# A two-layer graph kernel: layer 1 from the neighbour lists runs without a branch, and a branch behind it computes layer 1 from all of adj where the lists do not hold

## The chip, the core and the metric

One core of a Trainium2 chip runs one program. Its engines are PE (TensorE, matrix products), DVE (VectorE), ACT (ScalarE), POOL (GpSimd) and SP (SyncE, which issues DMAs here and computes nothing). Each engine runs its own instructions in a fixed order and waits at semaphores for the others; the order is what a scheduler makes of the kernel's source, except where `tc.keep_in_program_order` pins an instruction to its place in the source. The metric is device microseconds (us) of one execution, as the median of the runs.

## What is computed

4096 nodes with 512 features each, two layers. `adj` is 4096 x 4096; an entry is above zero for under 1% of the pairs, the diagonal among them, and its weights lie between 0.05 and 1.

```python
# layer 0
h = jnp.maximum(_layernorm(x, axis=-1), 0.0)
d = adj.sum(axis=1) ** -0.5            # 0 where the sum is 0
x = x + relu(((d[:, None] * adj * d[None, :]) @ h) @ W0 + b0)
# layer 1
h = jnp.maximum(_layernorm(x, axis=-1), 0.0)
g = h @ W1
e = leaky_relu(g @ a[:F] + (g @ a[F:]).T, 0.2)
pos =  softmax(where(adj > 0,  e, -1e12), axis=1)
neg = -softmax(where(adj > 0, -e, -1e12), axis=1)
x = x + elu(concatenate([pos @ h, neg @ h], axis=1) @ wtrans)
```

(The reference, written a little shorter.) Layer 1 needs for each node only the rows of h of its neighbours.

## The kernel before

**Layer 0** multiplies all of `adj` with h in dense form, in groups of row tiles of 128 nodes (`GROUPS`; `multiply_blocks`, L888 to L921, is its inner product; the rows of the profile name its matmuls L895). The last group holds the two tiles 24 and 25, called late. `finish0` (L807 to L828) finishes one tile: the residual, the layer norm with Relu on ACT (`normalize`, L640), two dot products on DVE (L818) which give the node's two score terms s and t, and `put_row`, which writes h, t and (elsewhere) the neighbour masks as a row to a table in DRAM. While layer 0 runs, DVE and POOL also make, for each block of 64 nodes, a list of all nodes that are a neighbour of one of them.

**Layer 1 from the lists** (`sparse_layer1`, from L1241 on) works on 64 blocks r of 64 nodes, two blocks to a pair n. `gather` issues indirect DMAs on POOL's queue (L457), each of which fetches 128 table rows that the lists name: a pair takes 22 of them, in three parts a = 0, 1, 2 of 8, 6 and 8 (`CHUNKS`). The even block of a pair uses parts 0 and 1, the odd block parts 1 and 2. Then per block:

- `weights`: scores s + t (DVE, L469), leaky relu (L475), exponentials of both signs (ACT, L479), masks (DVE, L486), a tree of sums over them (L491 to L497).
- `product`: 14 matmuls of 128 x 512 on PE, 28 records in the profile (L1303); the inverse sums scale the result on ACT (`us`, L1312); `turn_u` transposes it on PE (`tp`, L512).
- `finish1`, per pair: 8 matmuls with `wtrans`, 16 records (L1326), elu and residual, one store by SP (L1339).

Four to six gathers of a pair run ahead of its products, into buffers that alternate between pairs. `pause` (L447 to L451) is a copy on POOL, called `mark` in the profile, that waits until the last DMA of a gathered part has landed; it stands in the source behind part 1 of the first pair, part 0 of the second, and part 2 of the second to the sixth pair. The scheduler decides how many gathers of the next part stand between a part's own gathers and its mark.

**The early pair.** Pair 16 (blocks 33 and 32) is computed inside the last group of layer 0, before the late tiles are known: `gather0`, `weights0` and `product0` do the neighbours in the table, and `late_weights0` and `late_product0` add the late tiles' rows from SBUF. Layer 1 then begins with pair 17, whose blocks are 34 and 35.

**The verdict.** The lists have fixed lengths. `judge` (L1006 to L1032) tests whether every neighbour was listed, whether row sums are above zero and whether the scores are small enough for exponentials without a running maximum. It takes the minimum of the tests (`all_ok`), and a matmul with ones (`ok_ps`) adds it over the 128 partitions. Every engine loads the sum and branches: `sparse_layer1` where it is 128, `dense_layer1` where it isn't, which computes layer 1 from all of `adj`. For the data at hand every test holds.

The order around the seam in the source is: `weights0` of block 33 at step 10 of the last group and of block 32 at its last step; nine of the 14 chunks of block 33's product; `finish0` of the two late tiles; `judge`; the last five chunks; `spread_s`; block 32's product; the late parts; the branch; layer 1. Layer 1 opens with the load of four pairs' s (`load_s`, SP), the gathers of pairs 17 and 18, the load of `wtrans` to `wt_sb` (2 MB, SP) and, a block later, copies of table rows (SP).

Of the kernel before, what the change touches and what calls it, by code (L numbers as in the profile page):

```python
# [8 lines left out]
F32 = mybir.dt.float32  # L9
# [4 lines left out]
AF = mybir.ActivationFunctionType  # L14
ALU = mybir.AluOpType
AX = mybir.AxisListType
# [3 lines left out]
P = 128  # L20
# [239 lines left out]
def gcn_gat_kernel(  # L260
# [23 lines left out]
    nc = tc.nc  # L284
    N, F = x.shape
# [16 lines left out]
    late0, n_late = GROUPS[-1]  # L302
# [9 lines left out]
    def bank(name):  # L312
        return ps.tile([P, 512], F32, tag="ps", name=name)

    ones = const.tile([P, P], F32, name="ones")
# [154 lines left out]
            z, t.to_broadcast([P, n, RB]), s.unsqueeze(1).to_broadcast([P, n, RB]), ALU.add  # L470
        )

    def exps(z, p, bound=False):

        nc.vector.scalar_tensor_tensor(z, z, ALPHA, z, ALU.mult, ALU.max)  # L475
        if bound:
            nc.vector.tensor_scalar(z, z, 2 * MAXS, -2 * MAXS, ALU.min, ALU.max)
        for g in range(2):
            nc.scalar.activation(p[:, :, g, :], z, AF.Exp, scale=(1.0, -1.0)[g])  # L479

    def mask_out(r, p, mask):

# [38 lines left out]
    with sbuf(name="y0", bufs=1) as y_pool, sbuf(name="wa", bufs=1) as wa_pool, sbuf(name="bits", bufs=4) as bits_pool, sbuf(name="small0", bufs=4) as small, ExitStack() as rest, ExitStack() as lists:  # L521
# [108 lines left out]
        def normalize(out, xt, name, pin=False):  # L630

            mv = mean_var(small, xt, name, pin)
            r = small.tile([P, 2], F32, tag="rr", name=f"rr{name}")
            nc.vector.tensor_scalar(r[:, 0:1], mv[:, 1:2], EPS, None, ALU.add)
            nc.vector.reciprocal(r[:, 0:1], r[:, 0:1])
            nc.scalar.activation(r[:, 0:1], r[:, 0:1], AF.Sqrt)
            nc.vector.scalar_tensor_tensor(
                r[:, 1:2], mv[:, 0:1], -1.0, r[:, 0:1], ALU.mult, ALU.mult
            )
            nc.scalar.activation(out, xt, AF.Relu, bias=r[:, 1:2], scale=r[:, 0:1])  # L640

        def load_x(x_pool, queue, j):
            xs[j] = x_pool.tile([P, F], F32, tag="xt", name=f"xt{j}")
# [165 lines left out]
        def finish0(work, j, y, h, prod):  # L809

            xt = xrs.pop(j)
            nc.vector.scalar_tensor_tensor(y, y, 0.0, xt, ALU.max, ALU.add)
            nc.gpsimd.dma_start(out=x1_dram[j], in_=y)
            nc.gpsimd.memset(h[:, ROW_T + 1 :], 0.0)
            normalize(h[:, :F], y, f"b{j}")

            def dot(g, vec):
                nc.vector.scalar_tensor_tensor(  # L818
                    prod(f"prod{j}_{g}"), h[:, :F], 1.0, wa_bc[g], ALU.mult, ALU.mult, accum_out=vec
                )  # L820

            dot(1, h[:, ROW_T : ROW_T + 1])
            put_row(nc.gpsimd, tab0, j, h)
            if all(not j0 <= j < j0 + n for j0, n in GROUPS[-2:]):
                for g in others:
                    put_row(nc.scalar, g, j, h)
            dot(0, s_all[:, j : j + 1])
            nc.vector.tensor_copy(t_all[:, j : j + 1], h[:, ROW_T : ROW_T + 1])  # L828
# [176 lines left out]

        def judge():  # L1006

            ok = small.tile([P, 8], F32, tag="ok", name="ok", bufs=1)
            nc.gpsimd.memset(ok, 1.0)
            nc.vector.tensor_tensor(listed, listed, count, ALU.is_equal)  # L1010
            for g in range(2):
                nc.vector.tensor_reduce(ok[:, 4 + g : 5 + g], listed[:, g], AX.X, ALU.min)
            nc.vector.tensor_tensor(room[0], room[0], room[1], ALU.min)
            nc.vector.tensor_scalar(ok[:NH, 0:1], room[0], 0.0, None, ALU.is_ge)
            nc.vector.tensor_reduce(ok[:, 1:2], d_all, AX.X, ALU.min)
            nc.vector.tensor_scalar(ok[:, 1:2], ok[:, 1:2], 0.0, None, ALU.is_gt)
            for g, vec in enumerate((s_all, t_all)):
                sq = small.tile([P, NJ], F32, tag="sq", name=f"sq{g}", bufs=1)
                nc.vector.tensor_tensor(sq, vec, vec, ALU.mult)
                nc.vector.tensor_reduce(ok[:, 2 + g : 3 + g], sq, AX.X, ALU.max)  # L1020
                nc.vector.tensor_scalar(
                    ok[:, 2 + g : 3 + g], ok[:, 2 + g : 3 + g], MAXS * MAXS, None, ALU.is_le
                )
            all_ok = small.tile([P, 1], F32, tag="all_ok", name="all_ok", bufs=1)
            nc.vector.tensor_reduce(all_ok, ok[:, 0:7], AX.X, ALU.min)
            ok_ps = bank("ok_ps")
            tc.keep_in_program_order(
                nc.tensor.matmul(ok_ps[0:1, 0:1], all_ok, ones[:, 0:1], start=True, stop=True)
            )
            verdict = const.tile([1, 1], I32, name="verdict")  # L1030
            tc.keep_in_program_order(nc.vector.tensor_copy(verdict, ok_ps[0:1, 0:1]))
            return verdict  # L1032

        def group(b, work, at_pool, sum_pool, step, prod, n_h=2):
# [86 lines left out]
        with sbuf(name="work2", bufs=2) as work, sbuf(name="sums2", bufs=2) as sum_pool, sbuf(name="at2", bufs=4) as at_pool, sbuf(name="scratch", bufs=1) as scratch, sbuf(name="pair", bufs=1) as pair:  # L1121
            gts, ps0, totals, u0 = {}, {}, {}, {}
            blocks = (2 * PAIR0 + 1, 2 * PAIR0)
# [24 lines left out]
            def weights0(r):  # L1148
                nk = sum(CHUNKS[r % 2 : r % 2 + 2])
                z = scratch.tile([P, nk, RB], F32, tag="z", name=f"z{r}")  # L1150
                p = ps0[r] = pair.tile([P, nk + n_late, 2, RB], F32, name=f"p{r}")
                for gt, k, n in parts0(r):
                    scores(s_of0(r), z[:, k : k + n], gt[:, :, ROW_T : ROW_T + 1].bitcast(F32))
                exps(z, p[:, :nk], bound=True)
                for gt, k, n in parts0(r):
                    mask_out(r, p[:, k : k + n], gt[:, :, ROW_W:].bitcast(U8))
                q = p[:, :nk].rearrange("p k g c -> p k (g c)")
                totals[r] = tree(scratch, r, q, nk // 2, "z", 2)
# [14 lines left out]
            def product0(r, lo=0, hi=n_block):  # L1173
                if lo == 0:
                    u0[r] = bank(f"u{r}")
                for gt, k0, n in parts0(r):
                    for k in range(max(lo - k0, 0), min(hi - k0, n)):
                        i = nc.tensor.matmul(
                            u0[r],
                            ps0[r][:, k0 + k].rearrange("p g c -> p (g c)"),  # L1180
                            gt[:, k, :F].bitcast(F32),
                            start=k0 + k == 0,
                            stop=False,
                        )
                        if r == blocks[0]:
                            tc.keep_in_program_order(i)

            def late_product0(r):
                for k in range(n_late):
                    nc.tensor.matmul(  # L1190
                        u0[r],
                        ps0[r][:, n_block + k].rearrange("p g c -> p (g c)"),
                        late_h[:, k, :F],
                        start=False,
                        stop=k == n_late - 1,
                    )
                rl = inverse_sums(scratch, r, totals[r])
                u = xin.tile([P, F], F32, tag="xr", name=f"us{r}")
                nc.scalar.activation(u, u0[r], AF.Copy, scale=rl)
                turn_u(r, u, ut0)  # L1200

            def step(jp):
                if jp == 0:
                    nc.scalar.dma_start(
                        out=s_pair,
                        in_=s_dram[PAIR0 * P : (PAIR0 + 1) * P].partition_broadcast(P),
                    )
                if jp == 4:
                    gather0(1)
                if jp == 7:  # L1210
                    gather0(2)
                if jp == 10:
                    gather0(0)
                    weights0(blocks[0])
                if jp == NP - 1:
                    weights0(blocks[1])
                    warm = small.tile([P, 1], F32, tag="warm", name="warm2", bufs=1)
                    tc.keep_in_program_order(
                        nc.scalar.activation(warm, ones[:, 0:1], AF.Sqrt)
                    )  # L1220
# [4 lines left out]
                out=rows_of(tab0, late0 // EJ)[:, k : k + n_late, ROW_W:],  # L1225
                in_=late_m[:, k : k + n_late].bitcast(I32),
            )
            product0(blocks[0], hi=n_block - 5)
            for j, y in pending[1](work, row_tile).items():
                finish0(work, j, y, late_h[:, j - late0], row_tile)  # L1230
            verdict = judge()
            product0(blocks[0], lo=n_block - 5)
            spread_s(late0, n_late)
            product0(blocks[1])
            for r in blocks:
                late_weights0(r)
            for r in blocks:
                late_product0(r)


    def sparse_layer1():  # L1241
# [142 lines left out]
            turn(order[-1])  # L1384
            finish1(order[-1] // 2)

    go = nc.values_load(
        verdict[0:1, 0:1],
        min_val=0,
        max_val=P,  # L1390
        skip_runtime_bounds_check_because="a sum of 128 zeros and ones",
    )
    with tc.If(go == P) as branch:
        sparse_layer1()
    with branch.Else():
        dense_layer1(
            tc, adj_t, wtrans, out, x1_dram, table[tab0], s_all, t_all, ident, ones, load_adj_t, bank
        )
# [30 lines left out]
```

## Time and profile before

| | before |
|---|---|
| median of 3 runs | 2140.81 us (2140.43 to 2140.95) |
| profiled execution | 2128.36 us |
| its span | 2126.5 us |
| mean granted TensorE clock | 0.975 |
| DMA bytes, mean rate | 524.13 MB, 246 GB/s |

The page gives each engine's busy share over the span of one execution, a timeline, the chain of waits that ended last, and groups of instructions by line. Where the kernel's stages differ, a table of stretches of time says more than the shares: on this core layer 0 runs to about 1055 us, the early pair to about 1086 us, and layer 1 from there to the end. A group's mean hides where its instructions stand, so single instructions are read from the timeline of an engine. Its rows give the start in us, the length, the engine, the line, the operation with output and inputs, how many instructions were drawn together, and in brackets the idle time of the engine before them, with what ended it.

The costliest groups of layer 1, of the whole span:

```profile
L457 POOL DMA_INDIRECT g<-table,idx x704 | 742.6, 1055 | 261.6 <-issue 191.6
L1303 PE MATMUL u<-g,p 128*128 128x512 f32 x1736 | 764.8, 598 | 4.1 <-DVE p L486 4.1
L1326 PE MATMUL o<-wt_sb,ut 128*128 128x512 f32 x512 | 229.3, 601 | 0.5 <-ACT ut L516 0.5
```

The columns are the line, the engine, the operation and its number; busy time in us and the mean in ns; and the idle time before them with what ended most of it.

### The profile page before, as it was taken

To read this page: it belongs to the slowest core of one execution; us is meant where nothing else is said; L and a number is where in the kernel's file an instruction comes from. 1 tells how busy PE (TensorE), PEld (TensorE's weight loads), DVE (VectorE), ACT (ScalarE), POOL (GpSimd) and SP (SyncE) were. 2 spreads that over 40 slices of the span, in tenths; PEclk is the share of its full clock that TensorE was granted. 3 is DMA by queue.
4 is the path that set the end of the run, shared out by engine and by line. 5 is a ranking of instruction groups with operands and counts; after the bars stand their busy time and mean duration, and the time that the engine had idled before them with its cause. 6 is when DMAs were issued, how large, how long until landed. Compare 5 with 4: busy or idle time off the path is not lost.

```text
span 2126.5 us, 20058 instructions
## 1 busy us (share of the span) xinstructions
PE 2008.1 (94%) x6456; PEld 1184.0 (56%) x6456; DVE 1121.1 (53%) x2804; ACT 511.4 (24%) x876; POOL 915.8 (43%) x988
## 2 busy tenths in 40 slices
PE   7999899999899889899799999999999999999998
PEld 3444346888787768788544444444444444444443
DVE  5444436563797459935635435445445545445441
ACT  4645522223332310000112112122122122122120
POOL 2010001111112320321467667777777677677740
PEclk9999999999999999999899999999999999999999
DMA  9988926887887776464598878898888888888850
GB/s 373 364 313 311 347 84 231 303 274 223 309 276 256 254 241 208 129 221 136 163 309 248 251 227 257 285 296 256 276 253 264 254 271 246 237 247 241 238 167 21
DMA packets 188042, 524.13 MB, mean 246 GB/s; under 512 B 25235, under 2 KB 34419, under 8 KB 187926
## 3 DMA queue, kind: packets, MB, share of 16 engines
q0 software_dynamic: 71296, 275.22, 42.1%
q1 hardware_dynamic: 88480, 196.46, 27.1%
q10 hardware_dynamic: 28150, 51.07, 6.7%
q8 instruction: 52, 0.85, 0.2%
q14 instruction: 64, 0.52, 0.1%
HBM read 430.83 MB, written 102.92 MB: 251 GB/s over the span
## 4 chain that ended last, share of the span: by engine, by line
PE 47%; DVE 7%; DMA 5%; POOL 5%; issue 3%; ACT 1%; ACTq 0%; DVEq 0%; SPq 0%; POOLq 0%
PE u L1303 31%; PE o L1326 9%; PE p L895 5%; POOL g L457 5%; DMA g<-table,idx 2%; DMA at<-in_adj_t 2%; DVE keys L393 1%; DVE lst L391 1%; PE tp L512 1%; DMA table<-h 1%; ACT m L720 1%; DVE p L486 0%; DVE prod L818 0%; PE cs L502 0%; ACTq L443 0%
## 5 line engine op out<-in xcount | busy, mean ns | idle before, releaser
L457 POOL DMA_INDIRECT g<-table,idx x704 | 742.6, 1055 | 261.6 <-issue 191.6
L1303 PE MATMUL u<-g,p 128*128 128x512 f32 x1736 | 764.8, 598 | 4.1 <-DVE p L486 4.1
L1303 PEld LDWEIGHTS u<-g,p 128*128 128x128 f32 x1736 | 326.9, 191 | 393.3 <-issue 371.4
L469 DVE TENSOR_TENSOR z<-g,s 128x512 f32<-128x512 f32 (+1 forms) x124 | 77.4, 624 | 401.8 <-DMA g<-table,idx 365.4
L895 PE MATMUL p<-t,sums 128*128 128x256 f32 x832 | 249.4, 385 | 13.1 <-DVE sums L883 13.1
L895 PE MATMUL p<-y,sums 128*128 128x256 f32 x832 | 252.2, 385 | 6.6 <-DVE sums L885 6.6
L895 PE MATMUL p<-y,at 128*128 128x256 f32 x832 | 252.5, 386 | 2.9 <-DMA at<-in_adj_t 2.6
L1326 PE MATMUL o<-wt_sb,ut 128*128 128x512 f32 x512 | 229.3, 601 | 0.5 <-ACT ut L516 0.5
L479 ACT ACTIVATE p<-z 128x896 f32<-128x896 f32 (+2 forms) x136 | 116.0, 903 | 317.2 <-DVE z L475 287.2
L895 PEld LDWEIGHTS p<-t,sums 128*128 128x128 f32 x832 | 159.9, 193 | 37.0 <-DVE sums L883 15.0
L895 PEld LDWEIGHTS p<-y,sums 128*128 128x128 f32 x832 | 161.0, 194 | 30.1 <-DVE sums L885 7.4
L854 PE MATMUL acc<-y,at 128*128 128x512 f32 x384 | 174.9, 593 | 2.4 <-ACT y L706 2.4
L486 DVE SCALAR_TENSOR_TENSOR p<-g,p 128x384 f32<-128x384 uint8 (+1 forms) x256 | 143.4, 620 | 63.4 <-ACT p L479 60.4
L895 PEld LDWEIGHTS p<-y,at 128*128 128x128 f32 x832 | 159.2, 193 | 28.9 <-ACT m L720 3.0
L731 POOL DMA_DIRECT2D table<-m x71 | 54.1, 764 | 249.8 <-ACT m L720 145.6
L1326 PEld LDWEIGHTS o<-wt_sb,ut 128*128 128x128 f32 x512 | 96.4, 193 | 110.5 <-issue 109.8
L720 ACT ACTIVATE m<-at 128x1024 uint8<-128x1024 f32 (+1 forms) x110 | 105.2, 987 | 181.4 <-DMA at<-in_adj_t 132.7
L683 PE MATMUL yp<-w_sb,hx_t 128*128 128x512 f32 x256 | 125.0, 635 | 20.9 <-ACT y L706 18.4
L895 PE MATMUL p<-t,at 128*128 128x256 f32 x416 | 126.6, 387 | 18.9 <-DVE w L780 17.3
L1312 ACT ACTIVATE us<-u,rl 128x512 f32<-128x512 f32 x62 | 42.5, 686 | 382.2 <-issue 203.7
L854 PEld LDWEIGHTS acc<-y,at 128*128 128x128 f32 x384 | 70.5, 190 | 80.5 <-issue 77.6
L413 POOL DMA_INDIRECT ld<-li,off x48 | 43.9, 915 | 158.3 <-DMA ld<-li,off 108.1
(182 smaller groups left out, 1724.5 us busy)
## 6 DMA issues: line engine op xcount, KB each, us to landing
at<-in_adj_t SPq DMA_DIRECT2D x136, 512.0 KB, 5.4
ar<-in_adj SPq DMA_DIRECT2D x128, 512.0 KB, 8.7
table<-h ACTq DMA_DIRECT2D x182, 258.0 KB, 6.3
table<-m POOLq DMA_DIRECT2D x55, 256.0 KB, 5.5
at<-in_adj_t SPq DMA_DIRECT2D x32, 384.0 KB, 5.7
g<-table,idx POOLq DMA_INDIRECT x704, 4.2
xr<-in_x SPq DMA_DIRECT2D x32, 256.0 KB, 5.1
x<-x1d SPq DMA_DIRECT2D x32, 256.0 KB, 5.4
```

What stands on the lines that cost most here:

```text
L413: return nc.gpsimd.indirect_dma_start(out=lst_dram[g][:, :], out_offset=bass.IndirectOffsetOnAxis(ap=off[g][:, e, c : c + 1], axis=0), in_ ...
L457: nc.gpsimd.indirect_dma_start(out=gt[:, k, :], out_offset=None, in_=table[2 * n // RPT], in_offset=bass.IndirectOffsetOnAxis(ap=idx[n // ...
L469: return nc.vector.tensor_tensor(z, t.to_broadcast([P, n, RB]), s.unsqueeze(1).to_broadcast([P, n, RB]), ALU.add)
L479: nc.scalar.activation(p[:, :, g, :], z, AF.Exp, scale=(1.0, -1.0)[g])
L486: nc.vector.scalar_tensor_tensor(e, m, 0.0, e, ALU.is_gt, ALU.mult)
L683: nc.tensor.matmul(yp, hx_t[j][:, c * P : (c + 1) * P], w0_sb[:, c, :], start=c == 0, stop=c == FC - 1,)
L720: nc.scalar.activation(m, at, AF.Sign)
L731: nc.gpsimd.dma_start(out=rows_of(t, e)[:, c:, ROW_W + (a - t * TT) * P // 4 : ROW_W + (b - t * TT) * P // 4], in_=masks[i0][:, c:, (a - i ...
L854: nc.tensor.matmul(a, at[:, 0, it * P : (it + 1) * P], y0[j], start=j == 0, stop=j == NJ - 1)
L895: i = nc.tensor.matmul(out, left[:, x * P : (x + 1) * P], right, start=jp == 0 and first, stop=jp == NP - 1 and (final or not first),)
L1303: nc.tensor.matmul(u, p[:, k0 + k].rearrange("p g c -> p (g c)"), gt[:, k, :F].bitcast(F32), start=k0 + k == 0, stop=k0 + k == nk - 1,)
L1326: nc.tensor.matmul(po, ut[:, g, c, :], wt_sb[:, g * FC + c, :], start=g == 0 and c == 0, stop=g == 1 and c == FC - 1,)
```

## The change

1. `weights0` of block 32 moves from the last step of the group to behind `finish0` of the late tiles. ACT's Relu of the late tiles and its exponentials of the early pair are pinned to the source's order.
2. Block 33's product is one piece, and `judge` stands behind the early pair, unpinned. It now sums a flag for a failed test (`bad`): one more DVE instruction.
3. `sparse_layer1` runs without a branch. Behind it every engine loads the verdict, and `dense_layer1` runs where the sum is above zero; it then writes the output over.

```diff
-    def exps(z, p, bound=False):
+    def exps(z, p, bound=False, pin=False):
...
         for g in range(2):
-            nc.scalar.activation(p[:, :, g, :], z, AF.Exp, scale=(1.0, -1.0)[g])
+            i = nc.scalar.activation(p[:, :, g, :], z, AF.Exp, scale=(1.0, -1.0)[g])
+            if pin:
+                tc.keep_in_program_order(i)
...
-            normalize(h[:, :F], y, f"b{j}")
+            i = normalize(h[:, :F], y, f"b{j}")
+            if late0 <= j < late0 + n_late:
+                tc.keep_in_program_order(i)
...
-            all_ok = small.tile([P, 1], F32, tag="all_ok", name="all_ok", bufs=1)
-            nc.vector.tensor_reduce(all_ok, ok[:, 0:7], AX.X, ALU.min)
-            ok_ps = bank("ok_ps")
-            tc.keep_in_program_order(
-                nc.tensor.matmul(ok_ps[0:1, 0:1], all_ok, ones[:, 0:1], start=True, stop=True)
-            )
+            bad = small.tile([P, 1], F32, tag="bad", name="bad", bufs=1)
+            nc.vector.tensor_reduce(bad, ok[:, 0:7], AX.X, ALU.min)
+            nc.vector.tensor_scalar(bad, bad, 0.0, None, ALU.is_equal)
+            bad_ps = bank("bad_ps")
+            nc.tensor.matmul(bad_ps[0:1, 0:1], bad, ones[:, 0:1], start=True, stop=True)
             verdict = const.tile([1, 1], I32, name="verdict")
-            tc.keep_in_program_order(nc.vector.tensor_copy(verdict, ok_ps[0:1, 0:1]))
+            nc.vector.tensor_copy(verdict, bad_ps[0:1, 0:1])
...
-                exps(z, p[:, :nk], bound=True)
+                exps(z, p[:, :nk], bound=True, pin=True)
...
                 if jp == NP - 1:
-                    weights0(blocks[1])
...
-            product0(blocks[0], hi=n_block - 5)
+            product0(blocks[0])
             for j, y in pending[1](work, row_tile).items():
                 finish0(work, j, y, late_h[:, j - late0], row_tile)
-            verdict = judge()
-            product0(blocks[0], lo=n_block - 5)
+            weights0(blocks[1])
             spread_s(late0, n_late)
             product0(blocks[1])
             for r in blocks:
                 late_weights0(r)
             for r in blocks:
                 late_product0(r)
+            verdict = judge()
...
-    go = nc.values_load(
+    sparse_layer1()
+    bad = nc.values_load(
...
-    with tc.If(go == P) as branch:
-        sparse_layer1()
-    with branch.Else():
+    with tc.If(bad > 0):
         dense_layer1(
```

More of the change, by code (lines that the diff above doesn't have):

```diff
@@ L639, in normalize @@
             )
-            nc.scalar.activation(out, xt, AF.Relu, bias=r[:, 1:2], scale=r[:, 0:1])
+            return nc.scalar.activation(out, xt, AF.Relu, bias=r[:, 1:2], scale=r[:, 0:1])
         def load_x(x_pool, queue, j):
```

## The prediction

> **What bounds the kernel now.** I read the page's busy shares and its chain that ended last first, then a table of stretches from 1000 us on, then the timelines of PE, POOL and DVE from 1036 to 1300 us.
>
> ```profile
> PE 2008.1 (94%) x6456; PEld 1184.0 (56%) x6456; DVE 1121.1 (53%) x2804; ACT 511.4 (24%) x876; POOL 915.8 (43%) x988
> ```
>
> ```profile
> 1000.00:1040.00 40.00, 39.98 (x178) 33.11 (x177) 17.72 (x44) 4.35 (x6) 23.63 (x26) 1.00 0.78 246
> 1040.00:1062.00 22.00, 6.27 (x15) 2.66 (x14) 18.25 (x53) 6.90 (x11) 2.60 (x5) 0.70 0.15 55
> 1062.00:1090.00 28.00, 23.04 (x59) 10.15 (x57) 5.89 (x19) 4.81 (x13) 20.43 (x23) 0.93 0.81 244
> ...
> 1220.00:1300.00 80.00, 71.73 (x178) 32.86 (x178) 34.45 (x65) 15.68 (x27) 55.58 (x51) 0.94 0.79 238
> 1300.00:2100.00 800.00, 800.00 (x2083) 369.81 (x2082) 382.77 (x709) 160.46 (x271) 553.55 (x524) 1.00 0.80 245
> ```
>
> The columns are stretch, length, busy time (instructions) of PE, PEld, DVE, ACT and POOL, granted clock, DMA share and GB/s. PE is the bound almost everywhere: 39.98 of 40 us before 1040, 800 of 800 after 1300. The diff changes no matmul of the main stretches. It works on the seam, 1040 to 1062, where PE is busy 6.27 of 22 us and the clock falls to 0.70; what is won there must reach 1300 through a stretch where PE still waits.
>
> ```profile
> 1036.77 7.89 PE L1178 MATMUL u<-g,p 128*128 128x512 f32 x18
> 1060.39 0.19 PE L1028 MATMUL ok_ps<-ones,all_ok 128*1 128x1 f32 x2 [15.73 <-DVE all_ok L1025]
> ...
> 1067.89 12.28 PE L1178 MATMUL u<-g,p 128*128 128x512 f32 x28
> ...
> 1090.35 15.29 PE L1303 MATMUL u<-g,p 128*128 128x512 f32 x28 [4.06 <-DVE p L486]
> ```
>
> A row is start, length, engine, line, operation, and in brackets the idle time before it with its releaser. PE waits 15.73 us for the verdict's matmul, and 4.06 us for the first layer 1 weights. The same 28 matmuls take 15.29 us after that pause and 12.28 in the row above it: a cold start costs 3.0 to 3.2 us.
>
> ```profile
> 1058.84 0.54 POOL L443 DMA_DIRECT2D table<-late_h  x1 [1.78 <-DVE prod L818]
> 1062.30 1.00 POOL L457 DMA_INDIRECT g<-table,idx  x1 [2.92 <-DVE p L486]
> ...
> 1188.89 1.06 POOL L457 DMA_INDIRECT g<-table,idx  x1 [0.31 <-issue]
> 1190.61 0.18 POOL L450 COPY mark<-g 128x1 int32<-128x1 int32 x1 [0.67 <-DMA g<-table,idx]
> 1191.27 1.03 POOL L457 DMA_INDIRECT g<-table,idx  x1 [0.48 <-issue]
> ...
> 1217.31 0.95 POOL L457 DMA_INDIRECT g<-table,idx  x1 [0.30 <-issue]
> 1223.47 0.69 POOL L450 COPY mark<-g 128x1 int32<-128x1 int32 x1 [5.22 <-DMA g<-table,idx]
> 1224.32 1.77 POOL L457 DMA_INDIRECT g<-table,idx  x1 [0.16 <-DVE z L469]
> ...
> 1280.08 0.95 POOL L457 DMA_INDIRECT g<-table,idx  x1 [0.30 <-issue]
> ```
>
> From 1062 to 1296 POOL issues gathers back to back, one each 1.25 us (0.95 + 0.30), and stops only at its marks. A mark with two later gathers ahead of it stops the queue for 1.32 us (1189.95 to 1191.27); one directly behind its own gathers for 6.06 us (1218.26 to 1224.32), another like it for 8.44 (1253.58 to 1262.02).
>
> ```profile
> 1295.28 1.12 PE tp L512 x4
> ```
>
> In the chain of waits this PE step is the last that follows a stall: the gather issued at 1280.08 lands after 4.96 us, its scores start at 1285.16, and PE resumes at 1295.28 after 4.23 us idle. From there PE is dense to 2119.4. So the end is set by the POOL queue's position at 1280, not by PE's start at 1090, as long as PE arrives there with slack.
>
> **The change, part by part.** All against the profiled execution, 2128.36 us with a span of 2126.5; the median of the runs is 12.45 us more, which I carry over unchanged.
>
> *The late rows go first.* DVE stops doing block 32's masks (2.23) and tree (1.08 + 0.55 + 0.42 + 0.28) ahead of and among the late rows' steps, and their wait for ACT's exponentials (1.02) goes too: 5.6 us. The last table row leaves at 1053.2 instead of 1058.84. An end of 4.5 (the DVE work alone) would leave it 1.1 us later.
>
> *The branch in front leaves.* Between the last table row and the first gather lie 3.46 us in the trace; that row's write lands 2.3 us after issue. The rest bounds verdict load and branch from above at 1.2; ACT's idle time there, 0.35, from below. I take 0.6. First gather: 1062.30 - 5.6 - 0.6 = 1056.1.
>
> *Block 32's weights go behind.* ACT's second Relu ends at 1057.56 - 5.6 = 1052.0; table load 1.28, exponentials 1.79, first mask 0.56: PE starts block 32 at about 1055.7. Block 33's product is no longer split, so its 28 matmuls end at 1036.77 + 12.1 = 1048.9: PE idles 6.8 us instead of 15.73. Cold, block 32 costs 15.29 and ends at 1071.0; the late products and transposes took 6.27 (1080.01 to 1086.28), to 1077.3. Scores of block 34 wait for the row of s that is loaded behind block 33's late product; it moves with PE, so PE's first layer 1 product starts some 8 us earlier, near 1082.4, with a pause for its second part.
>
> *A new wait on POOL.* In the changed program pair 17's three gathers stand in the order third (8), first (8), second (6), and the second waits for the verdict's matmul, now behind PE's late transposes. Sixteen gathers end at 1056.1 + 16 x 1.25 = 1076.1; the wait lasts to 1077.6, 1.5 us. Behind it stand pair 18's first gathers and the mark, that is, everything POOL has left for layer 1. The mark, now after 24 gathers, waits for a gather issued at 1083.9: landing 4.03 as in the row of 1078.68, or 6.6 as for the gather of 1100.91 beside the loads of wtrans and the table copies, which in the changed order come some 9 us earlier and meet it. The 25th gather leaves between 1088.6 and 1091.3, before at 1094.05: -5.5 to -2.8. The next mark stopped POOL for 5.36 us (1104.57 to 1109.93) beside those loads; with them gone it costs 1.32, 4.0 less. Paid once, the contention leaves -5.5 to -6.8; paid twice, -2.8. I take -5, nearer the single payment.
>
> *One mark loses its cover.* The mark of pair 20 stands behind two gathers of pair 21 before and directly behind its own after. Price 6.06 - 1.32 = 4.7; by the dearer row 8.44 - 1.32 = 7.1. I take 4.7: the DMA share around it (0.83, 246 GB/s) is that of the nearer row. Pairs 21 and 22 have such marks in both.
>
> *The branch behind.* Every engine loads the verdict at its end and jumps over the dense version, some 8,400 instructions. PE, POOL, ACT and DVE do so while the last output lands (5.0 us in the median); SP waits for that landing and jumps twice where it jumped once. Nearest rows: 0.35 (ACT, branch not taken) and 2.9 (POOL's idle before the first gather, which holds a load and a branch). The 1.86 us around the span hold one jump. I take 1.5. The extra DVE step (0.15) of the verdict is hidden.
>
> [...] No row of before shows a taken jump alone.
>
> Sum at the gather of 1280.08: -5 + 4.7 = -0.3; with the tail +1.2. Profiled 2129.6, median 2140.81 + 1.2 = **2142.0 us**. Ends: -6.8 + 4.7 + 0.35 = -1.8 and -2.8 + 7.1 + 2.9 = +7.2, so this case's own range is 2139 to 2148.
>
> **Rivals.**
> 1. *The gain survives.* If the uncovered mark costs nothing because the landing it waits for would have held DVE and PE anyway (at 1223.43 the scores start within 0.04 us of the mark), the queue keeps -5, with the tail -3.5; if PE's 8 us also carry through, -6.5. Time 2134 to 2137, I say 2135.5. For it: PE idled 15.73 us and this is halved. Against: on POOL no gather after 1062 waits for anything but marks for long, so a stop adds to all behind.
> 2. *The verdict's matmul holds the gathers.* Should block 32's weights slip behind more DVE work (the dots, the verdict, block 33's late weights, which ended at 1062.5), PE starts late. At 1062.4 instead of 1055.7 the second gather of pair 17 waits 6.7 us more and the whole queue with it: -5 + 6.7 + 4.7 + 1.5 = +7.9, 2148.7. It passes 0.2% from a start of block 32 after about 1058.8. For it: before, that wait was over with the matmul at 1060.39, ahead of the first gather. Against: ACT's order is pinned, so exponentials follow the Relu at once.
> 3. *Nothing arrives.* PE's and POOL's shifts both vanish in PE's idle times and cold starts between 1090 and 1306 (3.2 + 5.4 + 0.6 + 5.1 + 0.2 + 7.5 us, row by row) and the mark finds cover: tail alone, 2142.3; it joins the forecast.
>
> **How the numbers follow.** About 0.2%, 4.3 us, is what a measurement tells from no change. Forecast and rival 3: 0.42. Rival 1: 0.27, mostly below 2136.5. Rival 2, with the dear end of the marks: 0.31, mostly above 2145.1. The range reaches to 2133 on the one side and 2149 on the other.
>
> **What would show it.** Right: last table row near 1053, first gather near 1056, PE's idle time before block 32 near 7 us, a POOL gap of 5 to 8 us at pair 20's mark, PE's last stall ending within 2 us of 1295.3. Wrong: a wait of over 4 us ahead of pair 17's last gathers (rival 2), or the last stall ending by 1291 (rival 1), or over 3 us between the last output's landing and the end.

## The result and the profile after

| | before | after |
|---|---|---|
| median of 12 runs each, in one comparison | 2139.64 us (2133.5 to 2145.8) | 2140.85 us (2134.91 to 2148.91) |
| ratio, 95% interval | | 1.0011 (0.9995 to 1.0027) |
| profiled execution, its span | 2128.36, 2126.5 us | 2135.61, 2133.8 us |
| span, from the start of PE's last 16 L1326 (after: L1329) matmuls to the end | 14.2 us | 15.3 us |

The change makes no difference that can be told: the interval of the ratio holds 1. The lines that answer to those shown of before, first the page's busy shares and the table of stretches (stretch, length, busy time and instructions of PE, PEld, DVE, ACT, POOL, clock, DMA share, GB/s); lines above 480 are 2 to 4 higher than before:

```profile
PE 2010.4 (94%) x6456; PEld 1184.6 (56%) x6456; DVE 1121.2 (53%) x2805; ACT 511.8 (24%) x876; POOL 923.9 (43%) x988
```

```profile
1040.00:1062.00 22.00, 20.34 (x49) 8.76 (x49) 17.52 (x57) 6.18 (x13) 9.74 (x11) 1.00 0.40 127
1062.00:1090.00 28.00, 13.98 (x37) 6.70 (x36) 3.60 (x10) 3.82 (x8) 16.95 (x18) 0.70 0.95 343
...
1220.00:1300.00 80.00, 73.93 (x188) 33.49 (x187) 35.85 (x70) 16.11 (x27) 55.07 (x52) 0.98 0.81 246
1300.00:2100.00 800.00, 794.29 (x2061) 366.42 (x2061) 382.40 (x707) 161.66 (x271) 558.96 (x523) 1.00 0.79 244
```

The seam is filled: PE is busy 20.34 of 22 us where it was 6.27. The idle time has moved one stretch on, where PE is now busy only 13.98 of 28 us, at a clock of 0.70. After 1300 the stretch that was full before has lost 5.7 us. PE's timeline shows both:

```profile
1037.67 12.18 PE L1182 MATMUL u<-g,p 128*128 128x512 f32 x28
1049.78 0.38 PE L837 MATMUL s_ps<-ident,s_all 128*2 128x128 f32 x2
1051.82 12.28 PE L1182 MATMUL u<-g,p 128*128 128x512 f32 x28 [1.66 <-DVE p L488]
...
1072.65 1.11 PE L514 MATMUL tp<-ident,us 128*128 128x128 f32 x4 [4.33 <-issue]
1073.69 0.19 PE L1033 MATMUL bad_ps<-ones,bad 128*1 128x1 f32 x2
1083.57 14.68 PE L1306 MATMUL u<-g,p 128*128 128x512 f32 x28 [9.69 <-DVE p L488]
...
1294.17 0.66 PE L514 MATMUL tp<-ident,us 128*128 128x128 f32 x4 [2.26 <-issue]
...
1311.43 1.45 PE L1306 MATMUL u<-g,p 128*128 128x512 f32 x3 [1.40 <-issue]
1313.54 1.28 PE L1306 MATMUL u<-g,p 128*128 128x512 f32 x2 [0.66 <-issue]
1315.63 0.59 PE L1306 MATMUL u<-g,p 128*128 128x512 f32 x1 [0.82 <-issue]
```

Block 33's product is in one piece, and PE's idle time before block 32's is 1.66 us, where 15.73 lay inside block 33's product. The early pair's last transposes end at 1073.76, 12.5 us sooner than before (5.2 us, counted from the origin that is used below, since layer 0 ended 7.3 us sooner in this execution). The stall that ended last before, at 1295.28, ends at 1294.17 here; from that origin this is 6.2 us later, not 1.1 sooner, and the row is marked "issue". Rows so marked hold idle time in which the engine waited for nothing that the profile shows; after 1310 one to three matmuls run every 2.1 us; the first profile of before has no such row for PE. They cost some 9 us between 1303 and 1324 alone, and hide what the change did. I call them holes; the experiments come back to them.

POOL's timeline:

```profile
1049.40 0.54 POOL L443 DMA_DIRECT2D table<-late_h  x1 [0.74 <-DVE prod L822]
1052.58 1.66 POOL L457 DMA_INDIRECT g<-table,idx  x1 [2.64 <-DMA table<-late_h]
...
1076.43 0.94 POOL L457 DMA_INDIRECT g<-table,idx  x1 [3.22 <-ACT ut L518]
...
1183.76 1.16 POOL L457 DMA_INDIRECT g<-table,idx  x1 [0.30 <-issue]
1188.57 0.18 POOL L450 COPY mark<-g 128x1 int32<-128x1 int32 x1 [3.65 <-DMA g<-table,idx]
1189.32 0.98 POOL L457 DMA_INDIRECT g<-table,idx  x1 [0.57 <-issue]
...
1224.48 0.69 POOL L450 COPY mark<-g 128x1 int32<-128x1 int32 x1 [5.19 <-DMA g<-table,idx]
```

The first gather now waits for the last table row's landing. The gather of 1076.43 is the first of pair 17's second part, held 3.22 us until ACT's last copy of the early pair. The mark of pair 20 now stops the queue from 1184.92 to 1189.32, 4.40 us, where it was 1.32.

### The profile page after: what moved, and what is told of

The parts are those of the page before. It is cut to its first block, busy times and chain, and to the rows that moved or that the text cites. A ratio compares the mean times of both kernels' runs of the same rounds, so it can differ in the third digit from the quotient of the medians.

```text
span 2133.8 us, 20055 instructions
## 1 busy us (share of the span) xinstructions
PE 2010.4 (94%) x6456; PEld 1184.6 (56%) x6456; DVE 1121.2 (53%) x2805; ACT 511.8 (24%) x876; POOL 923.9 (43%) x988
## 4 chain that ended last, share of the span: by engine, by line
PE 47%; DVE 6%; DMA 4%; POOL 4%; issue 3%; ACT 1%; ACTq 1%; another core or an unknown queue 0%; DVEq 0%; SPq 0%; POOLq 0%
PE u L1306 30%; PE o L1329 10%; PE p L899 5%; POOL g L457 4%; DMA at<-in_adj_t 2%; DMA g<-table,idx 1%; DVE keys L393 1%; PE tp L514 1%; DVE lst L391 1%; DMA table<-h 1%; ACTq L443 1%; PE u L1182 1%; ACT m L722 1%; DVE p L488 0%
## 5 line engine op out<-in xcount | busy, mean ns | idle before, releaser
L457 POOL DMA_INDIRECT g<-table,idx x704 | 753.4, 1070 | 266.6 <-issue 197.6
L1329 PE MATMUL o<-wt_sb,ut 128*128 128x512 f32 x512 | 230.5, 603 | 0.9 <-ACT ut L518 0.5
L1329 PEld LDWEIGHTS o<-wt_sb,ut 128*128 128x128 f32 x512 | 96.7, 194 | 111.9 <-issue 111.0
L886 DVE TENSOR_TENSOR sums<-at 128x256 f32<-128x256 f32 x104 | 43.3, 416 | 136.4 <-PE p L899 67.3
```

Of the source, the lines that this page charges most:

```text
L457: nc.gpsimd.indirect_dma_start(out=gt[:, k, :], out_offset=None, in_=table[2 * n // RPT], in_offset=bass.IndirectOffsetOnAxis(ap=idx[n // ...
L886: op(t[:, 0], a[:, :, 0, 1], a[:, :, 1, 1], ALU.add)
L1329: nc.tensor.matmul(po, ut[:, g, c, :], wt_sb[:, g * FC + c, :], start=g == 0 and c == 0, stop=g == 1 and c == FC - 1,)
```

## The experiments

Layer 0 ends at different times in different executions, so the profiles are compared from an origin inside them: G, the start of the early pair's last gather (1034.73 in the first profile of before, 1027.45 in that of the changed kernel). Ratios are to runs of the kernel before in the same set. Three sets of four kernels were run; before had medians of 2123, 2142 and 2140 us in them, so ratios are compared, not times. The four profiles of the first set (the kernel before again, without pair 20's mark, without the marks of pairs 21 and 22, and the weights moved alone) have no holes, as the first profile of before; all eight of the two other sets have them, as the first of the changed kernel.

### The kernel before, again

No edit.

> The kernel before once more, unchanged. Main theory (the POOL queue's position near 1280 us sets the end; front gain and dearer mark cancel): ratio 1.000 within 0.2%, and the profile again shows the mark of pair 20 with two gathers ahead of it (stop about 1.3 us) and those of pairs 21 and 22 without (6 to 8 us). On the holes of the changed kernel's profile, in which PE idles for nothing that the profile shows (4.33, 1.74, 2.26 us, and some 6 us between 1301 and 1319): if they belong to the changed program, this profile has none, as the first one of before had none; if they come and go by execution, it can have some, and spans differ by several us for the same program.

Measured: ratio 0.9999 (0.9986 to 1.0013). No hole on PE, and the same figures from G as the first profile: last table row +23.96 (+24.11), first gather +27.42 (+27.57), and POOL's 155th gather of layer 1, the first of pair 24 at 22 a pair, +257.55 (+257.96). The front is that stable; the span (2113.1 against 2126.5) is not, and neither are PE's stalls behind the front: its last 16 matmuls start at G + 1074.19 here and at G + 1077.54 in the first profile. So the end of a single profile is known to some 3 us only.

### The changed kernel without pair 20's mark

```diff
-                if (k, a) in ((0, 1), (1, 0)) or a == 2 and 0 < k < 6:
+                if (k, a) in ((0, 1), (1, 0)) or a == 2 and k in (1, 2, 4, 5):
                     pause(small, gt)
```

> The changed kernel without the mark of pair 20 (the pause alone is left out; every gather stands where it stood). Main theory: the mark stops POOL for about 4.7 us more than before, and POOL sets the end, so the time falls by 4 to 5 us against the changed kernel, to about 2136, ratio to before 0.998. Rival (the landing that the mark waits for holds DVE and PE anyway): no change, ratio 1.001.

Measured: ratio 0.9971 (0.9959 to 0.9983). Its profile has no holes either, so it shows the changed front undisturbed. Positions on POOL's queue, from G, in us:

| gather of layer 1 | before (2nd profile) | changed, without mark 20 | difference |
|---|---|---|---|
| 1st | 27.42 | 21.45 | -5.97 |
| 25th | 59.09 | 56.35 | -2.74 |
| 33rd, behind pair 18's mark | 74.71 | 70.77 | -3.94 |
| 89th, first of pair 21 | 153.38 | 151.24 | -2.14 |
| 97th | 165.31 | 162.64 | -2.67 |
| 155th | 257.55 | 253.34 | -4.21 |

```profile
1047.07 0.54 POOL L443 DMA_DIRECT2D table<-late_h  x1 [0.74 <-DVE prod L822]
1050.26 1.65 POOL L457 DMA_INDIRECT g<-table,idx  x1 [2.65 <-DMA table<-late_h]
...
1071.53 0.95 POOL L457 DMA_INDIRECT g<-table,idx  x1 [0.64 <-ACT ut L518]
```

In these rows of its POOL timeline the last table row leaves at G + 18.26 (before G + 23.96), and the wait ahead of pair 17's second part is only 0.64 us. So the front hands POOL 6.0 us, of which 2.1 arrive at pair 21; the rows below also hold the stop of 1.1 us at pair 20's mark that the kernel before still has. The main theory's direction holds. The runs are 0.0040 below the changed kernel's ratio of 1.0011, or some 8.5 us, with intervals that come to about 4 together; the expected 4 to 5 lies at the edge of that. The changed kernel itself was not in this set without holes, so the comparison goes across sets.

### The kernel before without the marks of pairs 21 and 22

The same line with `a == 2 and k in (1, 2, 3)`.

> The kernel before without the marks of pairs 21 and 22, which stop POOL for 6.06 and 8.44 us; nothing else moves. Main theory: all behind moves up until PE has no stall left to give; PE's idle times and cold starts from 1240 to 1306 are 0.6 + 5.1 + 0.2 + 7.5 = 13.4 us, so 10 to 13 us faster, ratio about 0.995. Rival (the marks only make visible a wait for landings that is there anyway): no change within 0.2%. A second rival: the marks keep the transfers apart, and without them gathers land later: slower.

Measured: ratio 0.9957 (0.9942 to 0.9973), 9.1 us faster, and the fastest ratio of all runs here. PE's timeline where it had 13.4 us of stalls and cold starts:

```profile
1236.29 12.26 PE L1303 MATMUL u<-g,p 128*128 128x512 f32 x28
1248.39 0.60 PE L512 MATMUL tp<-ident,us 128*128 128x128 f32 x4
1248.82 7.03 PE L1326 MATMUL o<-wt_sb,ut 128*128 128x512 f32 x16
...
1268.51 12.26 PE L1303 MATMUL u<-g,p 128*128 128x512 f32 x28
1280.61 0.60 PE L512 MATMUL tp<-ident,us 128*128 128x128 f32 x4
```

No row has an idle time in brackets; every product takes 12.26 us, and the 16 matmuls of L1326 take 7.03, where they took 8.66 and 9.56 behind two stalls in the first profile of before. From G, PE's last 16 matmuls start at 1065.38 us, against 1074.19 in the second profile of before: 8.8 us, and 12.2 against the first, around the 9.1 of the runs. The gathers land a little later for it, 4.7 us after issue in the median against 4.2 (from 1215 to 1320 and, in the second profile of before, from 1210 to 1315), which doesn't undo the gain. That POOL's position sets the end until PE is full is shown by this run for the marks of pairs 21 and 22; both rivals fall.

### The kernel before with block 32's weights moved alone

The move of `weights0(blocks[1])` behind `finish0`, and the pins; the branch in front, the verdict and the split product stay.

> The kernel before with one part of the change alone: block 32's weights behind the late tiles' rows, with the pins on ACT. Branch, verdict, split product and all marks stay as before. Main theory: the first gather comes 5 to 6 us earlier, and with pair 20's mark still covered the POOL queue carries 3 to 5 us to the end: about 2136, ratio 0.998. Rival (the front's gain is lost on the way whatever the marks do): 1.000.

Measured: ratio 0.9984 (0.9972 to 0.9997), 3.4 us faster. The last table row leaves at G + 18.26, as with the whole change, yet the first gather only at G + 25.40 instead of 21.45:

```profile
1049.43 0.54 POOL L443 DMA_DIRECT2D table<-late_h  x1 [0.74 <-DVE prod L822]
...
1054.89 0.15 DVE L1035 CAST verdict<-ok_ps 1x1 int32<-1x1 f32 x1
...
1056.57 1.00 POOL L457 DMA_INDIRECT g<-table,idx  x1 [6.60 <-DVE p L488]
```

POOL waits 6.60 us here, since the branch needs the verdict, which DVE makes behind block 32's masks in this order. The row names a mask that DVE ended just then, but in all five profiles with the branch in front the first gather starts 1.52 or 1.53 us after the end of the verdict (here 1055.04): so long the load of the verdict and the branch take on POOL's queue. So the move alone gives POOL 2.0 us, and the branch's absence the other 4: the two parts need each other. The 3.4 us of the runs can't be found at the end of the profile: the 155th gather comes at G + 255.47, 2.1 us earlier, but PE's last 16 matmuls start at G + 1074.69, between the two profiles of before.

### The changed kernel, again

No edit.

> The changed kernel once more, unchanged. If the holes of its first profile (PE idle for nothing that the profile shows, 1022 to 1028, 1072, 1301 to 1319) belong to that one execution, this profile has few or none of them, and its stages, counted from the first matmul of block 33 (S), read like those of the run without pair 20's mark up to that mark: last table row S + 16.2 us (before S + 22.0), first gather S + 19.4 (before S + 25.4), mark of pair 20 with a stop of 5 to 6 us, last stall of PE ending near S + 257 (before S + 258.3), no 1 to 2 us holes after 1300. If they belong to the program, they come again at the same matmuls. Ratio to before 1.001 within 0.2%.

Measured: ratio 1.0017 (1.0000 to 1.0035). The holes came again at about the same places (1018 to 1028, 4.44 us at 1073, 1300 to 1312), so the stages did not read as in a run without holes: that expectation failed.

### Without the marks of pairs 20, 21 and 22

The same line with `a == 2 and k in (1, 2)`, in the changed kernel.

> The changed kernel without the marks of pairs 20, 21 and 22; all gathers keep their order. Main theory (POOL's position sets the end until PE has no stall left): beyond the run without pair 20's mark, two stops of 5 to 6 us each go, but PE's stalls after 1240 were only 0.85 + 3.35 us and some 1.7 of cold start there, so 5 to 6 us more: ratio to before about 0.9945, PE without a stall after 1250. Rival (gathers that aren't held back land later, and PE stalls on them again): ratio 0.997 or above.

Measured: ratio 0.9969 (0.9953 to 0.9984): faster than the changed kernel of its set by 0.0048, some 10 us, which is about what the main theory gives the three marks together. Yet it is no better than without pair 20's mark alone in another set. The profile has 7 us of hole at the early pair's last transposes and more from 1212 to 1227. The figure is the rival's, but whether its reason is, or the holes are, can't be told from this profile.

### Block 32's weights back

`weights0(blocks[1])` at the last step again, in the changed kernel.

> The changed kernel with one part undone: block 32's weights back at the last step of the group, ahead of the late tiles. The rest (no branch in front, verdict behind, one piece product, marks) stays. Main theory: last table row near S + 22 instead of S + 16.2 and the first gather some 5 us later, which POOL carries to the end: 4 to 5 us slower than the changed kernel, ratio to before 1.003. Rival (POOL's wait for the verdict's matmul ahead of pair 17's last gathers takes the front's gain anyway, since PE is earlier then): within 2 us of the changed kernel.

Measured: ratio 1.0049 (1.0032 to 1.0065), about 0.0035 or 7 us above the changed kernel's two values so far, with intervals of 0.0017 on each. Its last table row leaves at G + 29.1, 5.3 us later than in the second profile of the changed kernel (G + 23.9), and POOL's 97th gather 6.6 us later. The rest of the change is worth nothing without the move: it costs.

### Without the dense version

The verdict is computed but not read, and `dense_layer1` is gone.

> The changed kernel without the branch behind and the dense version; the verdict is computed and not read, so lists that don't hold would go unnoticed. Main theory: the tail's price, about 1 us by the profile (7.3 us longer span with 6.3 us of it at PE's last matmul), ratio to before 1.0005. If the loads and jumps of the tail cost nothing: 1.001. Rival (a program that is smaller by some 8,400 instructions runs without the holes): 2 us or more faster than the changed kernel, and no holes in the profile.

Measured: ratio 0.9988 (0.9973 to 1.0003), 0.0029 below the changed kernel of its set. The holes are there all the same (7.43 us at 1076.58), so they don't come from the dense version's instructions. The part that the profile accounts for is the tail: from PE's last 16 matmuls to the end of the span 12.5 us, against 15.1 to 15.3 in every profile with the branch behind and 14.2 to 14.3 in every one with the branch in front. A branch behind costs 2.6 us, and 1.0 more than the one it replaced. The rest of the 0.0029, or 6 us, lies within the intervals. The DMA view of this stretch has eight packets on the queues of kind "instruction" in the first profiles of the changed kernel and of the kernel before (0.08 MB: 6 on q14, 2 on q8), and none without the branch.

### Before and after in one set

> The kernel before, a third time, in one set with the changed kernel and two variants, so that profiles of one chip stand side by side. Open: the holes (engines idle for nothing that the profile shows). Four profiles of the changed program on one chip have them near 1020 to 1030, 1073 and 1300 to 1320 us; all profiles of another chip, and the first of before, have none. If they follow the chip or the moment, this profile agrees with the next one: both have them or neither has. If they follow the program, this one has none and the next has them.

> The changed kernel, a third time, beside the kernel before. Main theory: from the same origin (the last gather of the early pair) the last table row leaves 5.6 us earlier than before (18.3 against 24.0 us where no hole lies between), pair 20's mark stops POOL for 5 to 6 us instead of 1.3, and the last stall of PE ends within 3 us of before's. Ratio 1.001 within 0.2%. With holes in both or in neither, as said for the run before.

Measured: 0.9994 (0.9983 to 1.0004) and 1.0009 (0.9993 to 1.0025). Both profiles have holes. PE's timeline of the kernel before, in this execution:

```profile
1023.62 0.58 PE L895 MATMUL p<-y,sums 128*128 128x256 f32 x1 [1.02 <-issue]
1025.06 0.59 PE L895 MATMUL p<-y,sums 128*128 128x256 f32 x1 [0.85 <-issue]
...
1086.05 1.12 PE L512 MATMUL tp<-ident,us 128*128 128x128 f32 x4 [3.82 <-issue]
...
1103.61 1.11 PE L512 MATMUL tp<-ident,us 128*128 128x128 f32 x4 [16.22 <-issue]
```

So the change doesn't cause the holes. Whether they go with the execution, the moment or the chip stays open: within a set, all profiles have them or none has, and the set without them is the one with the median of 2123 us. Side by side, the last table row is at G + 29.6 before and G + 23.9 after, 5.7 us; the 97th gather at G + 172.99 and G + 173.48; the span ends at G + 1105.2 and G + 1105.6. What the front won is gone at pair 21, and the end is 0.4 us apart.

### The verdict's flag in a buffer of its own

```diff
-            bad = small.tile([P, 1], F32, tag="bad", name="bad", bufs=1)
+            bad = const.tile([P, 1], F32, name="bad")
```

> The changed kernel with the verdict's flag in a buffer of its own, so that pair 17's second part need not wait for the verdict's matmul; the scheduler then also puts that part ahead of the first one. Main theory: POOL's wait ahead of it (3.2 to 4.5 us with holes at the early pair's transposes, 0.6 us without) goes, and POOL carries that to pair 20: 3 us faster than the changed kernel with holes, within 1 us without. Rival: the first part, now last, comes so late that PE's first product starts 3 to 5 us later, and this is what counts: no gain, or slower.

Measured: ratio 0.9988 (0.9976 to 1.0000), 0.0021 or 4.5 us below the changed kernel of its set, about as much as the two intervals come to together. The wait ahead of pair 17's second part is gone. In the profile the 17th gather comes at G + 48.1 instead of 51.0 and the 89th at G + 159.0 instead of 162.7. PE's first product of layer 1 starts at 1096.70, G + 68.1, where the changed kernel of this set has G + 55.5: 12.6 us later, most of it in one hole. The kernel is no slower for it.

### And without three marks

> The last one, and without the marks of pairs 20, 21 and 22. Main theory: both gains add as far as PE has stalls: ratio to before 0.994 to 0.996. Rival (PE's stalls between 1100 and 1240 are set by the first products' late start, not by the marks): 0.997, as without the marks alone.

Measured: ratio 0.9966 (0.9953 to 0.9978): 0.0022 below the same kernel with its marks, between the two expectations. It beats both kernels, but not the kernel before without two marks (0.9957), whose interval it overlaps, in another set.

## Why the prediction was right

The forecast was no difference, 2142.0 us, 1.2 above the median; measured were ratios of 1.0011, 1.0017 and 1.0009, 2 to 4 us. It was right for its main reason, a gain at the front that POOL's queue carries on and gives back by pair 20's mark and at the tail. But the sizes differ: by the profiles it is -2.1 at pair 21's first gather, +3 for the mark and +1.0 for the tail, +1.9 in all, where the forecast had -5, +4.7 and +1.5. That its sum came so close is in part luck. Its steps:

- **The late rows go first: -5.6 us.** 5.7 in the pair without holes (23.96 to 18.26) and in the pair with them (29.57 to 23.91). The second agreement is in part chance, since with holes the row leaves anywhere from G + 21.9 to G + 26.1 in the other profiles that have the move.
- **First gather: -6.2.** -5.97 without holes, -5.76 with them. The branch in front was worth 0.3 of that, not 0.6 (from the last row's issue to the first gather 3.46 us before, 3.19 after). Nor does the bound of 1.2 hold: load and branch take 1.53 us behind the verdict, which ended 0.4 us ahead of the row's landing, and 0.87 us pass between landing and gather without a branch too (changed kernel without mark 20). And the small price holds only where the verdict is ready; with the move alone, its wait cost 4 us.
- **PE's pause before block 32: 6.8.** 4.25 + 1.84 = 6.1 in the run without holes.
- **PE's first layer 1 product 8 us earlier.** Wrong: 3.4 (from G, 55.39 before, 52.00 in the changed kernel without mark 20). The working moved the load of s with PE and forgot that pair 17's first part is now gathered second: its scores start at 1077.35 in the changed kernel without mark 20, 7.4 us after its last gather's issue, released by a gather's landing, beside the load of `wtrans`. It didn't matter, since PE's start doesn't set the end; the kernel with the flag in its own buffer started 12.6 us later and was no slower.
- **The wait ahead of pair 17's second part: 1.5.** 0.64 without holes, 3.2 to 3.4 in the changed kernel's three profiles, where the transposes themselves are held. But it isn't the verdict's matmul that is waited for, as forecast and the second rival had it: the gather waits for a semaphore of ACT and starts 0.1 to 0.2 us after ACT's last copy of the early pair in these four profiles, 0.8 to 3.0 after the matmul's end. The run with the flag in a buffer of its own has no such wait, and also another order of the parts; what moved the wait there isn't shown.
- **POOL at the 25th gather -5.5 to -2.8, at the 33rd -5.** -2.7 and -3.9: the dear end first, then a second stop (3.41 us behind pair 18's mark) that was cheaper than before's 5.41 but not free: the two stops are 3.58 + 3.41 us against 1.33 + 5.41. By pair 21 only 2.1 of the 6.0 are left; the 1.8 us lost between the 33rd and the 89th gather come in small steps, and no single wait explains them.
- **Pair 20's mark: +4.7.** Stops of 4.4, 5.0 and 4.2 us in three profiles against 1.3, 1.1 and 1.9: about 3 us. The term was too dear, and the one before it too generous; that the errors cancel is luck. The dearer row, 8.44, was also misread: a gather stands at 1253.88, so the stop is 7.2 us (1254.83 to 1262.02), and the upper end of the range should have been 2146.8, not 2148.
- **The tail: +1.5.** +1.0: from PE's last 16 matmuls to the end of the span 15.1 to 15.3 us with the branch behind, 14.2 to 14.3 with the one in front. With neither it is 12.5, so a branch behind costs 2.6 us. In the first profiles of both kernels this stretch has eight packets on the queues of kind "instruction", without a branch none; how much of the 2.6 us goes with them isn't shown. No run shows a taken jump alone, and the 1.5 was my estimate between 0.35 and 2.9.

The first rival, that the gain survives, would have shown as a stall ending by 1291; it ended at 1294.17, but with layer 0 shorter by 7.3 us and in a hole, so this sign says nothing for itself. What speaks against the rival is the pair of profiles with holes, where nothing is left of the gain at the 97th gather. Its argument, that the landing which the mark waits for is waited for anyway, fell with the marks of pairs 21 and 22, whose removal won 9 us. The third rival, that nothing arrives, was half true: two thirds of the front's gain were gone by pair 21, but the mark found no cover. In time it can't be told from the forecast.

## What to carry to other kernels

Where a queue that never rests feeds an engine, ask where in that queue a gain stands, not how much sooner the engine starts: here a first product that started 12.6 us later cost nothing that could be seen, while two stops of POOL's queue, 11.3 us above its usual spacing, cost 9.1. What a wait costs that was put in to pace transfers depends on how many later transfers stand ahead of it (here, with two of them at pair 20's mark, 1.1 to 1.9 us, with none 4.2 to 7.2), and a scheduler may change that number with an edit elsewhere; compare the order of such queues before and after. And count stages from an event inside the profile, since spans of one program differed here by 19 us; even then, the same program's last matmuls came 3.4 us apart in two profiles without holes.

## What the runs showed that I had not expected

Engines stand idle for nothing that the profile shows, in some executions of the same program and not in others: there is no such row on PE in two profiles of the kernel before, and one of 16.22 us at a transpose in the third. At the same place ACT takes up at 1097.51 a transpose that PE had ended at 1087.17, and DVE at 1084.87 a sum that was ready at 1080.4. They come at similar places (1020 to 1035, the early pair's end, 1300 to 1324), one or a few matmuls every 1.4 or 2.1 us. In the three profiles of the changed kernel no packet on the queues of kind "instruction" overlaps a hole of over 0.3 us on PE; in the third of before one of 0.3 us, at 1088.5, falls into the hole of 16.22. What causes them stays open.
